# A 7x7 depthwise convolution taken image by image, as two matrix products for tiles of sixteen by two pixels

## The chip, the cores and the metric

One NeuronCore of one Trainium2 chip runs the whole program. The metric is the device time of one execution in microseconds (us). Engines: TensorE (PE; its weight loads are PEld), VectorE (DVE), ScalarE (ACT), GpSimd (POOL), and SyncE (SP), which here only issues transfers.

## The reference, cut to what matters

The input `x` is 4 images of 256 channels and 64 x 64 pixels, in float32. Two layers follow each other, each added to its input. Layer A is an attention whose keys and values come from a 2x2 convolution with stride 2. Layer B is an attention within each quarter of an image (16 rows, 1024 pixels), to which a 7x7 convolution of the values is added before the last projection:

```python
def _L1_conv_ref(x, w_qkv, b_qkv, w_pe, b_pe, w_proj, b_proj):
    ...
    qkv = _conv1x1(x, w_qkv, b_qkv)            # q, k, v: 8 heads of 32
    ...
    attn = softmax(einsum('bihd,bjhd->bhij', q, k) * scale)   # in one quarter
    out = einsum('bhij,bjhd->bihd', attn, v)
    ...
    out = out + _dwconv7(v_full, w_pe, b_pe)   # each channel by itself, 7 x 7
    return _conv1x1(out, w_proj, b_proj)

x = x + _L0_conv_ref(_gn(x), ...)              # layer A
x = x + _L1_conv_ref(_gn(x), ...)              # layer B
```

## The kernel before, in words

**Units and steps.** The work is written as a sequence of 128 units: 16 for each of the 8 pairs of layer and image, first A for images 0 to 3, then B for images 0 to 3. So layer A is units 0 to 63, layer B of image b is units 64 + 16b to 79 + 16b. A unit is 4 heads by 512 queries. It has 8 steps, one for each 128 keys; there are 1024 steps. Each step is the same on TensorE: four products for the scores (`s`, line 261), and the four weighted sums (`av`, line 272) of the step before. ScalarE makes two exponentials of 128 x 1024 in each step (line 265), VectorE adds up the exponentials for the divisors (line 797). Once in a unit, four `den` products (line 281) make the divisors, and GpSimd's transfers carry their reciprocals.

**Side work.** Everything else is hung on this frame. `at(g, j, f)` calls `f` in unit g, step j. Work of TensorE is queued with `task(parts, f)`: a generator cut in parts. After its own products, each step takes one part from this first-in-first-out queue (two if more than 7 parts wait, three beyond 14, and one less where j is 2). `need` takes parts ahead of time where a result is wanted at once. The order of all engines' instructions is that of this program (`manual_schedule`), SP's transfers included: an instruction at the head of an engine's queue that waits holds all that stand behind it.

**Values.** `plan_values(b, c)` makes the values of eight rows of image b: it loads `hv`, normalizes it on ScalarE, multiplies (`vals_ps`, two tasks of two parts), and adds the bias on ScalarE into `vout`. `vout` goes to HBM twice: as `vala` for attention (read as `vc`, and transposed on VectorE by `make_v`), and as `vals`, rows of all four images side by side with a margin of zeros.

**The convolution.** `plan_conv(n)` takes four channels of all four images. Its matrices are bands: the vertical taps are in the 126 x 32 matrix (42 rows of the image for each of three horizontal shifts; `BAND`, `BROWS`), and three such products cover seven columns. It loads six pieces of `vals` into `rows` (line 705), for every second n three pieces of `bands` (line 717), and does 24 products of 256 columns (line 732) in three parts. `HD` is 32: each product fills 32 columns of the array, and four of them, m = 0 to 3, stand beside each other. The result is copied by ScalarE (`cout`, line 739) and stored in `conv` (line 741). The convolutions wait for the values of all images: they are due at `begin` = unit 70.5 and every 0.52 units, 64 in all.

**The projections.** Therefore the attention output of images 0 to 2 is stored (`attd`, line 548), and read back with `conv` (lines 556 and 562) from unit 105.3 on, every 0.8 units: `add_conv` adds both on VectorE (line 572), and `project` (two tasks of two parts, `ops`) multiplies and adds the residual `xm` (line 583). For image 3 it follows attention directly.

Of the kernel before, what the change touches and what calls it, by code (L numbers as in the profile page):

```python
# [15 lines left out]
P = 128  # L16
# [17 lines left out]
BAND = HH // 2 + 2 * HALO  # L34
BROWS = 42
TC = 8
# [18 lines left out]
def direct_path(  # L55
# [31 lines left out]
    attd = [[dram.tile([P, CT, CH], FP, name=f"attd_{b}_{c}") for c in range(NCH)] for b in range(B - 1)]  # L87

    vals = dram.tile([HH + 2 * HALO + BROWS - BAND, C, B, XP], FP, name="vals")

    vala = [[dram.tile([4, HD, NH, 4, XP], FP, name=f"vala_{b}_{a}") for a in range(NAREA)] for b in range(B)]
    conv = dram.tile([C, B, N], FP, name="conv")

    bands = dram.tile([C // TC, 9, BROWS + HH // 2 - 1, TC], FP, name="bands")
# [369 lines left out]
    def plan_b(b, u):  # L464
# [13 lines left out]
        def make_k(a, qd, half):  # L478
            if qd == 0 and half == 0:
                kvs["k"] = k_tile(("B", b, a))  # L480
            k, ps = kvs["k"], ps_side(f"k1ps_{b}_{a}_{qd}_{half}")
            for t in range(CT):
                product(
                    ps, lhsT=wqkv_sb[:, t, 1, qd * P : (qd + 1) * P],
                    rhs=hs[a][:, t, half * CH : (half + 1) * CH], start=(t == 0), stop=(t == CT - 1),
                )
                if t == 0:
                    yield

            S.activation(  # L490
                k[:, qd, :].rearrange("p (j t i) -> p t j i", t=4, i=32)[:, 2 * half : 2 * half + 2],
                ps.rearrange("p (t j i) -> p t j i", t=2, i=32), AF.Identity, bias=bqkv_sb[:, 1, qd : qd + 1],
            )
            if qd == 1 and half == 1:
                ks["B", b, a] = k

        def load_v(a, half):
            vcs[a, half] = pool.tile([P, NH // 2, 4, XP], FP, tag="vc", name=f"vc_{b}_{a}_{half}", bufs=2)
            nc.sync.dma_start(
                vcs[a, half], vala[b][a][:, :, half * NH // 2 : (half + 1) * NH // 2].rearrange("t c h r x -> (t c) h r x")  # L500
            )

        def make_v(a, half):

            if half == 0:
                kvs["v"] = v_tile(("B", b, a))
            v, vc = kvs["v"], vcs.pop((a, half))
            V.transpose(
                out=v[:, :, half * P : (half + 1) * P].rearrange("p (r j) (h c) -> p h r j c", j=2, c=HD),
                in_=vc[:, :, :, HALO : HALO + WW].rearrange("p h r (j w) -> p h r j w", w=HD),  # L510
            )
            if half == 1:
                vs["B", b, a] = v
# [17 lines left out]
        for a in range(NAREA):  # L531
# [6 lines left out]
            for half in range(2):  # L538
                at(g - 3, 2 + 5 * half, lambda a=a, half=half: load_v(a, half))
                at(g - 2, 2 + 4 * half, lambda a=a, half=half: make_v(a, half))  # L540
# [5 lines left out]

        def store_att(c):
            nc.sync.dma_start(attd[b][c], atts.pop(("B", b, c)))
# [5 lines left out]
        def load_rest(c):  # L554
            cv = chunk_tile(f"cv_{b}_{c}")
            nc.sync.dma_start(cv, conv[:, b, c * CH : (c + 1) * CH].rearrange("(t p) n -> p t n", p=P))
            att = None
            if c == NCH - 1:
                load_residual(c)
            if b < B - 1:  # L560
                att = chunk_tile(f"at_{b}_{c}")
                nc.sync.dma_start(att, attd[b][c])
            rest[c] = cv, att

        def add_conv(c):
            cv, att = rest[c]
            if c < NCH - 1:
                load_residual(c)
            if att is None:
                att = atts["B", b, c]  # L570
            for t in range(CT):
                V.scalar_tensor_tensor(cv[:, t, :], cv[:, t, :], bpe_sb[:, t : t + 1], att[:, t, :], ALU.add, ALU.add)

        def project(c, to):
            cv, ps = rest[c][0], ps_side(f"ops_{b}_{c}_{to}")
# [7 lines left out]
            V.scalar_tensor_tensor(xm[:, to, :], ps, bproj_sb[:, to : to + 1], xm[:, to, :], ALU.add, ALU.add)  # L583
# [4 lines left out]

        for c in range(NCH):
            g, j = u + 2 * c + 3, 5  # L590
            if b < B - 1:
                at(g, j + 1, lambda c=c: store_att(c))
                g, j = 0, int(NKT * (late + spread * (b * NCH + c)))
            else:
                at(g, j, lambda c=c: add_conv(c))
                at(g, j + 2, lambda c=c: soon_tasks([(2, project, c, to) for to in range(CT)]))
                g, j = (g - 1, 5) if c < NCH - 1 else (g - 2, 2)
            at(g, j, lambda c=c: load_rest(c))
            if b < B - 1:
                at(g, j + 4, lambda c=c: add_conv(c))  # L600
                at(g, j + 6, lambda c=c: soon_tasks([(2, project, c, to) for to in range(CT)]))
# [13 lines left out]

    def plan_zeros(g):


        def zeros():
            zero = pool.tile([P, 8 * B * XP], FP, tag="rows", name="zero", bufs=2)  # L620
            V.memset(zero, 0.0)
            for lo, hi in ((0, 3), (67, 71), (71, 74)):
                nc.sync.dma_start(
                    vals[lo:hi].rearrange("r c b x -> (r c b x)").rearrange("(p n) -> p n", n=8 * B * XP),
                    zero[: (hi - lo) * C // 8],
                )
            flat = bands.rearrange("k x i c -> (k x i c)").rearrange("(p n) -> p n", p=P)
            nc.sync.dma_start(flat, zero[:, : flat.shape[1]])

        def taps():  # L630
            tap = pool.tile([NTAP, C], FP, tag="cout", name="tap", bufs=2)
            nc.sync.dma_start(tap, wpe.rearrange("c k -> k c"))
            for n in range(7):
                nc.sync.dma_start(
                    bands[:, :7, BAND - 1 - n, :].rearrange("k x c -> x k c"),
                    tap[7 * n : 7 * n + 7, :].rearrange("x (k c) -> x k c", c=TC),
                )

        at(g, 0, zeros)
        at(g, 2, taps)  # L640
# [3 lines left out]
    def plan_values(b, c, start):  # L644
# [10 lines left out]
        def values(t):  # L655
            if t == 0:
                vout = made["v"] = pool.tile([P, CT, RC, XP], FP, tag="rows", name=f"vout_{b}_{c}", bufs=2)
                V.memset(vout[:, :, :, :HALO], 0.0)
                V.memset(vout[:, :, :, HALO + WW :], 0.0)
            h, vout = made["h"], made["v"]  # L660
            ps = ps_side(f"vals_ps_{b}_{c}_{t}")
            for tt in range(CT):
# [7 lines left out]
                vout[:, t, :, HALO : HALO + WW], ps.rearrange("p (r w) -> p r w", w=WW), AF.Identity,  # L670
                bias=bqkv_sb[:, 2, t : t + 1],
            )
            if t == CT - 1:
                stored[b, c] = True
                for n in range(2):
                    for tt in range(CT):
                        nc.sync.dma_start(
                            vala[b][c // 2][2 * (c % 2) + n, :, 4 * tt : 4 * tt + 4].rearrange("c h r x -> h c (r x)"),
                            vout[:, tt, 4 * n : 4 * n + 4, :].rearrange("p r x -> p (r x)"),
                        )  # L680
                for r in range(RC):
                    nc.sync.dma_start(
                        vals[HALO + HH - 1 - c * RC - r, :, b, :].rearrange("(t p) x -> p t x", p=P), vout[:, :, r, :]
                    )
# [8 lines left out]
    band_tiles = {}  # L693

    def plan_conv(n, start):

        made = {}

        def load():
            row, size = C * B * XP, 4 * B * XP  # L700
            need(stored, (B - 1, NCH - 1))
            made["x"] = xs = pool.tile([3 * BROWS, 2, 4, B, XP], FP, tag="rows", name=f"rows_{n}", bufs=2)
            for half in range(2):
                for s in range(3):
                    nc.sync.dma_start(
                        xs[s * BROWS : (s + 1) * BROWS, half].rearrange("p c b x -> p (c b x)")[:, : size - s],
                        bass.AP(
                            tensor=vals.tensor, offset=vals.offset + (1 - half) * (HH // 2) * row + n * size + s,
                            ap=[[row, BROWS], [1, size - s]],
                        ),  # L710
                    )
            k, part = divmod(4 * n, TC)
            if part == 0:
                band = band_tiles[k] = pool.tile([3 * BROWS, 3, HH // 2, TC], FP, tag="band", name=f"band_{k}", bufs=2)
                step = (BROWS + HH // 2 - 1) * TC
                for s in range(3):
                    nc.sync.dma_start(
                        band[s * BROWS : (s + 1) * BROWS].rearrange("p g y c -> p g (y c)"),
                        bass.AP(
                            tensor=bands.tensor, offset=bands.offset + (9 * k + s) * step,  # L720
                            ap=[[TC, BROWS], [3 * step, 3], [1, HH // 2 * TC]],
                        ),
                    )

        def convolve():
            xs, (k, part) = made.pop("x"), divmod(4 * n, TC)
            ps = ps_side(f"conv_ps_{n}").rearrange("p (i b x) -> p i b x", i=2, b=B)
# [716 lines left out]
```

## Time and profile before

| | us |
|---|---|
| median of 3 runs (lowest to highest) | 3266.19 (3265.86 to 3269.84) |
| the profiled execution, as timed | 3270.47 |
| its span, first to last instruction | 3268.7 |
| TensorE busy, 29730 matmul records | 3218.2 |
| ScalarE busy | 2525.6 |
| VectorE busy | 2491.6 |
| GpSimd busy | 487.2 |

A float32 matmul of the program appears as two records, so a part of eight products is 16 records. `128*32` is rows by columns of the weights. A row of the timeline shows: start in us, length in us, engine, line, operation, tiles, shape, how many records, and in brackets the idle time before it and what ended it. A row of the windows shows, for a stretch of time, the busy us of each engine and its number of instructions, then the granted share of TensorE's clock, the busy share of the 16 DMA engines, and GB/s.

### The profile page before, as it was taken

Reading aid. Unit: us, or ns where it says so; the run is one execution under the profiler, and the core shown is the slowest. Engines: PE = TensorE matmul, PEld = TensorE weight load, DVE = VectorE, ACT = ScalarE, POOL = GpSimd, SP = SyncE. Lnnn points to the kernel's source line nnn. Section 1 sums busy time; section 2 is a strip of 40 time slices with the busy share of each in tenths; the row PEclk is TensorE's granted clock in tenths of the full one; section 3 lists DMA queues with packets and bytes.
Section 4 is the critical chain, followed back from the end, with each engine's and each line's share of the span. In section 5 each row is a group of like instructions: output and inputs, shape, how many; then the busy total and the mean of one; then the engine's idle time right before and its main releaser. Section 6 shows DMA issues by size and latency. Waiting matters only on the chain.

```text
span 3268.7 us, 72561 instructions
## 1 busy us (share of the span) xinstructions
PE 3218.2 (98%) x29730; PEld 961.1 (29%) x29730; DVE 2491.6 (76%) x2621; ACT 2525.6 (77%) x2993; POOL 487.2 (15%) x923
## 2 busy tenths in 40 slices
PE   7999999999999999999999999999999999999997
PEld 4233323333233322222222333333333322222221
DVE  3777897779877787778876767666776778888887
ACT  3888788887888888888887777777777787776765
POOL 0111121111211111111111111111111111111111
PEclk9999999999999999999999999999999999999999
DMA  5312212313322213553236667676766643445431
GB/s 179 80 64 73 77 66 90 100 59 116 100 69 84 65 63 91 148 138 113 82 120 158 162 151 178 159 174 141 180 171 153 172 142 123 166 147 172 155 121 57
DMA packets 319853, 397.27 MB, mean 122 GB/s; under 512 B 182652, under 2 KB 215708, under 8 KB 319192
## 3 DMA queue, kind: packets, MB, share of 16 engines
q1 hardware_dynamic: 291064, 356.06, 38.5%
q0 software_dynamic: 28448, 36.48, 4.2%
q8 instruction: 236, 3.87, 0.5%
q14 instruction: 105, 0.86, 0.1%
HBM read 285.98 MB, written 106.42 MB: 120 GB/s over the span
## 4 chain that ended last, share of the span: by engine, by line
PE 94%; DMA 2%; issue 1%; ACT 1%; DVE 1%; SPq 0%; POOL 0%; DVEq 0%; ACTq 0%; POOLq 0%
PE s L261 33%; PE av L272 29%; PE conv_ps L732 5%; PE den L281 4%; PE k0ps L155 3%; PE k1ps L155 3%; PE q1ps L155 3%; PE v0ps L155 3%; PE q0ps L155 3%; PE ops L155 3%; PE vals_ps L155 3%; ACT p L265 1%; DVE p L797 1%; DMA conv<-cout 0%; DMA rows<-vals 0%
## 5 line engine op out<-in xcount | busy, mean ns | idle before, releaser
L797 DVE TENSOR_TENSOR p<-p 128x1024 f32<-128x1024 f32 x1792 | 2113.3, 1219 | 623.1 <-ACT p L265 583.3
L265 ACT ACTIVATE p<-s 128x1024 f32<-128x1024 f32 x2048 | 2016.9, 1027 | 571.9 <-PE s L261 564.0
L261 PE MATMUL s<-q,k_A 32*128 32x512 f32 x4096 | 608.2, 640 | 1.4 <-ACT p L265 0.9
L261 PE MATMUL s<-q,k_B 32*128 32x512 f32 x4096 | 588.7, 640 | 1.1 <-ACT p L265 0.8
L272 PE MATMUL av<-p,v_A 128*32 128x512 f32 x4096 | 551.1, 603 | 0.0
L272 PE MATMUL av<-p,v_B 128*32 128x512 f32 x4096 | 546.0, 604 | 0.0
L308 POOL DMA_DIRECT2D rb<-recs x508 | 252.4, 502 | 454.1 <-DMA recs<-few 377.5
L306 POOL DMA_DIRECT2D recs<-few x127 | 70.2, 553 | 1423.2 <-DVE sums L305 1372.1
L261 PEld LDWEIGHTS s<-q,k_A 32*128 32x128 f32 x4096 | 176.3, 183 | 357.8 <-issue 273.3
L261 PEld LDWEIGHTS s<-q,k_B 32*128 32x128 f32 x4096 | 162.5, 182 | 363.3 <-issue 290.5
L272 PEld LDWEIGHTS av<-p,v_A 128*32 128x32 f32 x4096 | 89.4, 108 | 383.0 <-issue 335.0
L272 PEld LDWEIGHTS av<-p,v_B 128*32 128x32 f32 x4096 | 87.6, 108 | 378.8 <-issue 332.9
L732 PE MATMUL conv_ps<-rows,band 126*32 126x256 f32 x3072 | 195.1, 379 | 0.0
L732 PEld LDWEIGHTS conv_ps<-rows,band 126*32 126x32 f32 x3072 | 123.0, 139 | 113.0 <-issue 78.3
L297 POOL DMA_DIRECT2D rows<-den_sb x127 | 74.6, 587 | 433.3 <-ACT den_sb L290 424.1
L281 PE MATMUL den<-p,ones 128*32 128x512 f32 x1024 | 137.8, 605 | 0.4 <-DVE p L797 0.4
L155 PE MATMUL ops<-cv,wp_sb 128*32 128x512 f32 x1024 | 129.8, 600 | 6.0 <-issue 6.0
L155 PE MATMUL vals_ps<-hv,wqkv_sb 128*32 128x512 f32 x1024 | 130.1, 596 | 3.9 <-ACT vout L669 3.8
L155 PE MATMUL k0ps<-taps,wk_sb 128*32 128x256 f32 x2048 | 130.6, 383 | 3.0 <-ACT taps L243 3.0
L155 PE MATMUL k1ps<-h,wqkv_sb 128*32 128x512 f32 x1024 | 128.7, 593 | 2.4 <-ACT cout L739 1.6
L155 PE MATMUL q0ps<-hq,wq_sb 128*32 128x512 f32 x1024 | 129.8, 592 | 0.0
L155 PE MATMUL q1ps<-h,wqkv_sb 128*32 128x512 f32 x1024 | 129.7, 596 | 0.1
(87 smaller groups left out, 1594.9 us busy)
## 6 DMA issues: line engine op xcount, KB each, us to landing
rb<-recs POOLq DMA_DIRECT2D x508, 64.0 KB, 2.4
rows<-vals SPq DMA_DIRECT2D x128, 189.0 KB
rows<-vals SPq DMA_DIRECT2D x128, 188.8 KB
rows<-vals SPq DMA_DIRECT2D x128, 188.7 KB
vala<-vout SPq DMA_DIRECT2D x128, 144.0 KB
vals<-vout SPq DMA_DIRECT2D x256, 72.0 KB
vc<-vala SPq DMA_DIRECT2D x32, 576.0 KB
hq<-in_x SPq DMA_DIRECT2D x32, 512.0 KB
```

The lines of the kernel that those rows point to most:

```text
L155: T.matmul(out[cols, :], lhsT=lhsT[:, cols], rhs=rhs, start=start, stop=stop)
L261: T.matmul(pairs[h // 2][:, h % 2, :], lhsT=k[rows, unit[0], j * P : (j + 1) * P], rhs=q[rows, :], start=True, stop=True,)
L265: exps = [lambda i=i: S.activation(p[i], pairs[i], AF.Exp, scale=SCALE) for i in range(2)]
L272: T.matmul(av[HD * h : HD * h + HD, :], lhsT=v[:, j, unit[0] * P + HD * h : unit[0] * P + HD * h + HD], rhs=p[h // 2][:, h % 2, :], start= ...
L281: T.matmul(dens[g][HD * h : HD * h + HD, :], lhsT=ones, rhs=p[h // 2][:, h % 2, :], start=True, stop=True,)
L297: G.dma_start(rows, den_sb[0:P:HD, :])
L306: G.dma_start(recs.rearrange("h (q n) -> (h q) n", n=CH // HD), few[:, 1, :])
L308: G.dma_start(rb[HD * h : HD * h + HD, :], recs[h : h + 1, :].to_broadcast([HD, CH]))
L732: T.matmul(ps[HD * m : HD * m + HD, i], lhsT=band_tiles[k][:, g, :, part + c], rhs=xs[:, m % 2, c, :, 3 * g : 3 * g + WW], start=(g == 0), ...
L797: soon(1, lambda i=i: V.tensor_add(ps[0][i], ps[0][i], ps[j][i]))
```

## The change

The convolution is done for one image at a time. A product now makes tiles of sixteen rows by two columns (`TY`, `TX`; 32 pixels, so again 32 columns of the array): its 88 rows hold 22 image rows, by two even/odd columns, by two shifts. Two products cover 22 rows and 8 columns of input. One n is 16 channels of one image: 32 products of 128 columns, in two parts. `vals` of each image holds even and odd columns apart (`f`), and so do `vala`, the keys and `conv`. The matrices are built once in HBM (`mats`, by 8 reads and one store for each of 32 k) and read for each image; `load_rows` reads two of them and eight pieces of `vals` for one n. It is called for n + 1 at the end of `convolve(n)`, behind the copy of the result and its store. `conv` is read by 16 transfers for each chunk of eight rows. The projections of all images follow their attention, as those of image 3 did; `attd` is gone. The values are stored for each 128 channels by themselves, in `vc` buffers, of which there are five; they and the convolutions have new due times.

```diff
-BAND = HH // 2 + 2 * HALO
-BROWS = 42
-TC = 8
+TY, TX, NY, XT, NP, TC = 16, 2, 4, WW // 2 + 4, 88, 8
+BY, BX = 2 * 16 + 5, 2 + 7
...
-        def load_v(a, half):
-            vcs[a, half] = pool.tile([P, NH // 2, 4, XP], FP, tag="vc", name=f"vc_{b}_{a}_{half}", bufs=2)
...
+        def load_v(a, n):
+            vcs[a, n] = pool.tile([P, 2, 4 * TX, XT], FP, tag="vc", name=f"vc_{b}_{a}_{n}", bufs=5)
...
         def load_rest(c):
             cv = chunk_tile(f"cv_{b}_{c}")
-            nc.sync.dma_start(cv, conv[:, b, c * CH : (c + 1) * CH].rearrange("(t p) n -> p t n", p=P))
...
+            for y in range(c * RC, (c + 1) * RC):
+                n, r = y // TY, TY - 1 - y % TY
+                for t in range(CT):
+                    nc.sync.dma_start(
+                        cv[:, t, :].rearrange("p (f r x) -> p r f x", f=TX, r=RC)[:, y - c * RC],
+                        conv[b][t * P : (t + 1) * P, r * TX : (r + 1) * TX, n, :],
+                    )
...
-            if b < B - 1:
-                at(g, j + 1, lambda c=c: store_att(c))
-                g, j = 0, int(NKT * (late + spread * (b * NCH + c)))
...
+            at(*((g - 1, 5) if b < B - 1 or c < NCH - 1 else (g - 2, 2)), lambda c=c: load_rest(c))
+            at(g, j, lambda c=c: add_conv(c))
+            at(g, j + 2, lambda c=c: soon_tasks([(2, project, c, to) for to in range(CT)]))
...
+        def matrices(k):
+            band = pool.tile([NP, 2, TY, TX * TC], FP, tag="band", name=f"made_{k}", bufs=2)
+            for dc in range(TX + 6):
+                p = NP // 2 * (dc // 2 % 2) + dc % 2
+                nc.sync.dma_start(
+                    band[p : p + 2 * (TY + 6) - 1 : 2, dc // 4],
...
+            nc.sync.dma_start(mats[k], band)
...
+            at(g + 2, 3 * k, lambda k=k: matrices(k))
...
-                vout = made["v"] = pool.tile([P, CT, RC, XP], FP, tag="rows", name=f"vout_{b}_{c}", bufs=2)
...
+            vout = pool.tile([P, RC, TX, XT], FP, tag="vc", name=f"vout_{b}_{c}_{t}", bufs=5)
...
+    def load_rows(b, n):
+        for c in range(NCH):
+            need(stored, (b, c))
+        loaded[b, n] = made = []
+        row, size = C * XT, 8 * XT
+        for k in (2 * n, 2 * n + 1):
+            band = pool.tile([NP, 2, TY, TX * TC], FP, tag="band", name=f"band_{b}_{k}", bufs=2)
+            xs = pool.tile([NP, 2, NY, 8, XT], FP, tag="rows", name=f"rows_{b}_{k}", bufs=2)
+            made.append((band, xs))
+            nc.sync.dma_start(band, mats[k])
+            for a in range(4):
+                p = NP // 2 * (a % 2)
+                nc.sync.dma_start(
+                    xs[p : p + NP // 2, a // 2].rearrange("p y c x -> p y (c x)")[:, :, : size - 3],
+                    bass.AP(
+                        tensor=vals[b].tensor, offset=vals[b].offset + k * size + a,
+                        ap=[[row, NP // 2], [TY * TX * row, NY], [1, size - 3]],
+                    ),
+                )
...
+    def convolve(b, n):
+        size = NY * WW // TX
+        ps = ps_side(f"conv_ps_{b}_{n}")
+        for k, (band, xs) in enumerate(loaded.pop((b, n))):
+            if k:
+                yield
             for i in range(2):
-                for g in range(3):
+                for half in range(2):
                     for m in range(4):
...
                         T.matmul(
...
+                            lhsT=band[:, half].rearrange("p y (x c) -> p (y x) c", c=TC)[:, :, 4 * i + m],
+                            rhs=xs[:, half, :, 4 * i + m, : WW // TX], start=(half == 0), stop=(half == 1),
                         )
...
+        S.copy(out.rearrange("p i y -> p (i y)"), ps)
+        nc.sync.dma_start(
+            conv[b][16 * n : 16 * n + 16].rearrange("(i c) m y x -> (c m) i (y x)", i=4), out
+        )
+        if n + 1 < C // 16:
+            load_rows(b, n + 1)
+        yield
...
-        at(0, when, load)
-        at(0, when + 4, lambda: task(3, convolve))
...
+        if n == 0:
+            at(0, when - 8, lambda: load_rows(b, n))
+        at(0, when, lambda: task(2, convolve, b, n))
...
-            plan_values(b, c, ends[b] + 1.8 + (14.5 if b == 1 else 0) + (3.4, 1.0, 1.6, 0.4)[b] * c)
-    for n in range(C // 4):
-        plan_conv(n, begin + pace * n)
+            plan_values(b, c, (17.8, 42, 54.5, 67)[b] + (2.0, 1.5, 1.3, 2.2)[b] * c)
+        for n in range(C // 16):
+            plan_conv(b, n, (36, 58, 75.5, 93.5)[b] + (1.36, 1.06, 1.1, 1.1)[b] * n)
```

## The prediction

> **What bounds the kernel now.** First the page: engines, then the chain of work that ended last.
>
> ```profile
> span 3268.7 us, 72561 instructions
> PE 3218.2 (98%) x29730; PEld 961.1 (29%) x29730; DVE 2491.6 (76%) x2621; ACT 2525.6 (77%) x2993; POOL 487.2 (15%) x923
> ...
> PE 94%; DMA 2%; issue 1%; ACT 1%; DVE 1%; SPq 0%; POOL 0%; DVEq 0%; ACTq 0%; POOLq 0%
> ```
>
> TensorE is the bound, and the other two compute engines have a quarter of the span free. Busy overstates TensorE, so I read the price of side work off the timeline, from one `s` group to the next. TensorE in layer B, then three rows of a stretch without side work:
>
> ```profile
> 2190.46 1.14 PE L261 MATMUL s<-q,k_B 32*128 32x512 f32 x8
> ...
> 2192.41 1.92 PE L732 MATMUL conv_ps<-rows,band 126*32 126x256 f32 x32
> 2194.26 1.14 PE L261 MATMUL s<-q,k_B 32*128 32x512 f32 x8
> ...
> 2196.22 1.06 PE L732 MATMUL conv_ps<-rows,band 126*32 126x256 f32 x16
> 2197.20 1.14 PE L261 MATMUL s<-q,k_B 32*128 32x512 f32 x8
> ```
> ```profile
> 3212.04 1.31 PE L261 MATMUL s<-q,k_B 32*128 32x512 f32 x8
> ...
> 3214.28 1.14 PE L261 MATMUL s<-q,k_B 32*128 32x512 f32 x8
> ...
> 3216.35 1.31 PE L261 MATMUL s<-q,k_B 32*128 32x512 f32 x8
> ```
>
> A step with two convolution parts takes 3.80 us, with one 2.94, with none 2.07 to 2.24: **a part costs 0.87 us**, and 192 of them 167 us. In an empty step ScalarE's two exponentials (2 x 1.03 us) set the pace. Thus time is nearly a count of parts, plus the waits of TensorE.
>
> How a product's time is made, by the tile view of `conv_ps` (count, then shortest, median and longest ns):
>
> ```profile
> L732 PEld LDWEIGHTS conv_ps<-rows,band x3072: 135/138/164, 1797.9 to 2653.0; 126*32 126x32 f32 x192
> L732 PE MATMUL conv_ps<-rows,band x3072: 377/379/435, 1797.9 to 2653.2; 126*32 126x256 f32 x192
> ```
>
> Four products stand beside each other, so a part (16 records) is four groups of 0.218 us for 256 columns. The longest, 435 ns, is 56 over the median: I read it as a group whose weights were not loaded ahead.
>
> How fast a load comes: SP's timeline, and the windows over the same load (1.13 MB of `rows`, 0.39 MB of `band`):
>
> ```profile
> 2218.71 2.45 SPq L705 DMA_DIRECT2D rows<-vals  x6
> 2221.21 1.37 SPq L717 DMA_DIRECT2D band<-bands  x3
> ```
> ```profile
> 2218.70:2220.00 1.30, 1.30 (x12) 0.35 (x16) 1.30 (x2) 1.30 (x3) 0.00 (x0) 1.00 0.29 53
> ...
> 2222.00:2223.00 1.00, 1.00 (x12) 0.16 (x8) 1.00 (x2) 0.48 (x2) 0.00 (x0) 1.00 0.83 193
> ...
> 2226.00:2227.00 1.00, 1.00 (x20) 0.60 (x16) 0.32 (x1) 0.99 (x2) 0.00 (x0) 1.00 0.96 209
> 2227.00:2228.00 1.00, 1.00 (x20) 0.35 (x12) 0.00 (x0) 1.00 (x2) 0.00 (x0) 1.00 0.30 47
> ```
>
> The last two columns say it: a slow first 1.3 us, then some 200 GB/s until about 2227. Its matmuls begin at 2229.37, 10.7 us after the first issue, without a wait. Last, what a stall costs beyond itself:
>
> ```profile
> 1281.45 1.94 PE L155 MATMUL vals_ps<-hv,wqkv_sb 128*32 128x512 f32 x8 [3.15 <-ACT vout L669]
> 1283.32 1.67 PE L261 MATMUL s<-q,k_A 32*128 32x512 f32 x8
> ```
>
> After the wait, eight records take 1.94 us instead of 1.04, and the next group 1.67 instead of 1.14: about 1.5 us more.
>
> [...]
>
> **The change, part by part.**
>
> *Convolution products.* 192 parts of four 256-column groups go; 128 parts of eight 128-column groups come (4 images x 16 n x 2). If columns set the time, a group takes half of 0.218, a part again 0.87 us: 64 x 0.87 = **56 us less**. A load of 56 ns fits under a group of 109 ns. No group this short is in the trace. If weights lay fully bare, 1024 groups x 56 ns = 57 us would come back and nothing be saved; a faster side I exclude, since columns and clock stay. I take 56. The steps left without side work, counted in both program orders, are 88 and 84: 4 x 0.17 = 0.7 us less.
>
> *The load behind the convolution.* New: `load_rows(b, n + 1)` stands in SP's queue behind the copy and store of `convolve(n)`. In the changed program's order, the 64 blocks' first part stands this many steps behind its load: 0 for three blocks, 1 for one, 2 for two, 3 for one, 4 or more for 57. Before, load and task were planned four steps apart. Counting from the step's start: copy 0.6 and store issue 0.65, with their hand-overs 1.4 us. A k brings 0.18 MB of `mats` and 0.80 MB of `vals`; at 200 GB/s that is 4.9 us, and fixed 2.1 (1.3 as above, 0.8 after the last byte: a 64 KB `rb` lands in 2.4 us on the page, of which 0.3 is its bytes). So the first k is there at 8.4 us, the second at 13.3. TensorE comes to the part 1.95 us into its step. Same step: 6.4 us of waiting, then 2.0 more at the second part, 8.4 x 3 = 25 us. One step: 3.5 + 2.0. Two steps: 0.6 + 4.0 where both parts stand in one step, else 0.6. Three or more: none. Sum 36 us; with five clock drops of 1.6, **44 us more**. Behind the waiting product are the next scores, and so ScalarE and everything. Ends: nothing, if these steps come late[...]. I take 44.
>
> *Values.* `vout` gets five buffers for two. TensorE's weight loads of `vals_ps` waited 9.9 us for `vout`, and products behind `cout` 1.6 (waits): **11 us less**. Late next would be the same buffers, shared with `vc`: ends 0 and 15 less.
>
> *SP's queue.* The order counts 1418 transfers before, 2143 after; `rows` takes a median of 0.38 us to issue. (a) `conv` for a chunk: 16 x 0.38 = 6 us plus landing, with 4 to 11 steps (12 us and more) until VectorE needs it; ten buffers of `p` cover some lateness. (b) `matrices`: nine issues 3.5 us, then the store waits some 2 us for the reads, every three steps (8.8 us) in units 4 to 14, where `xa` and `hq` loads queue behind it with 4 or 5 steps of lead. (c) `attd` and its reads, 48 transfers, go. All this is covered by lead unless SP runs late: 0 to 15 us, I take **4 more**.
>
> *VectorE and ScalarE.* The sums by column (128 of 0.75 us), twice as many memsets and half-size transposes, the even/odd reads in `vout` and the keys (128 of 0.69). Were the strided ones twice as slow, either engine would gain some 90 us and still stand under 81% of the span: hidden by TensorE, except four at the very end, 0 to 3 us. I take 0. Keys, projections and values keep their number of products; 64 copies of `cout` stay 64.
>
> Sum: -56 - 1 + 44 - 11 + 4 = **-20 us** on the profiled execution's 3270.5 (span 3268.7 and 1.8 around it), so 3250.5. That execution is 4.3 above the median of 3266.2: **3247**.
>
> **The rivals.**
>
> *R1, slower: the load comes late.* At 140 GB/s the wait is 76 us: -56 - 1 + 76 - 11 + 4 = +12, 3278. [...] It decides from 71 us of waiting on, just under 9 us for a first k.
>
> *R2: weights show.* The short groups wait for their weights: +57 on the forecast, 3304; half of it, 3275. For it: 56 ns is half of the 109. Against: in the 256-column groups nothing of it is seen.
>
> *R3: the load is in time.* If the tight blocks wait less than 10 us in all, -56 - 1 + 10 - 11 + 4 = -54, 3212. For it: TensorE may reach those steps late. Against: the ones in the same step have less than 2 us.
>
> *R4: nothing is saved for want of filler*, since empty steps are paced by ScalarE: 64 parts would then have to leave empty steps, but these do not grow (88 to 84). It would give 3266 less the values' 11, and I give it little.
>
> **How the numbers follow.** Forecast 0.50, 3215 to 3262, nearly all faster; R1 0.20; R2 0.12; R3 0.13; R4 and others 0.05. A measurement of this kernel tells apart about 0.2%, 6.5 us. Faster: 0.48 + 0.13 + a little of the rest, 0.62; the same, the edge between forecast and R1, 0.14; slower 0.24. The range takes in R3's 3212 with 5 us to spare and most of R2: 3207 to 3290.
>
> **What would show it.** Right: `conv_ps` has 4096 records and some 135 us busy; `conv_ps` waits for DMA `rows`, about 36 us on fewer than ten occasions, in units 71, 87, 95 and 107 above all; no wait for `vout`; steps with one part still 2.94 us. Wrong: one-part steps of 3.1 us or more (R2); waits for `rows` under 10 us (R3) or over 70 (R1); ScalarE waiting for `xa` or `hq`, which I priced at 4 us.

## The result, and the profile after

| | before, us | after, us |
|---|---|---|
| median of 7 runs (lowest to highest) | 3269.4 (3265.9 to 3272.3) | 3287.5 (3281.0 to 3300.5) |
| the profiled execution, as timed | 3270.5 | 3287.5 |
| its span | 3268.7 | 3285.4 |
| granted TensorE clock, mean | 0.997 | 0.987 |

The changed kernel is **slower by 0.6%**: ratio 1.0061, 95% interval 1.0043 to 1.0080. The forecast was 3247, faster by 20 us; it came 18 slower. Its own runs lie up to 20 us apart, so a difference of a few us from it is not told apart.

The page of after: the engines, the chain that ended last by engine, and the group of the convolution's products.

```profile
span 3285.4 us, 75646 instructions
...
PE 3182.4 (97%) x30754; PEld 965.8 (29%) x30754; DVE 2508.6 (76%) x2717; ACT 2524.9 (77%) x2993; POOL 491.2 (15%) x923
...
PE 87%; DMA 6%; issue 2%; DVE 2%; ACT 1%; SPq 1%; POOL 0%; DVEq 0%; ACTq 0%
...
L742 PE MATMUL conv_ps<-rows,band 88*32 88x128 f32 x4096 | 143.0, 282 | 44.9 <-DMA rows<-vals 44.8
```

TensorE is busy 36 us less and the span is 17 us longer: the work went down, the waiting went up. The last two lines say where to look first. TensorE's share of the chain fell from 94% to 87%, that of transfers rose from 2% to 6%, and the convolution's products stood still for 44.8 us for `rows`. The tile view of `conv_ps` (count, then shortest, median and longest ns) shows the products themselves: a median of 272 ns at 128 columns, where before had 379 at 256.

```profile
L742 PEld LDWEIGHTS conv_ps<-rows,band x4096: 135/138/178, 969.4 to 2870.2; 88*32 88x32 f32 x196
L742 PE MATMUL conv_ps<-rows,band x4096: 270/272/432, 969.8 to 2870.3; 88*32 88x128 f32 x196
```

On the timeline, groups of four products follow each other every 0.109 us, half of the 0.218 of 256 columns and as forecast, and a step with one convolution part takes 2.94 us, as before.

**Where the time went.** For both traces I took each step from its first `s` product to the next step's, and counted what it takes over the usual time of a step with the same side work. This puts each stall under the step in which it falls:

| us over the usual, steps with | before | after | difference |
|---|---|---|---|
| convolution | 0.3 | 63.3 | +63.0 |
| divisors (`den`) | 3.0 | 16.9 | +13.9 |
| projections (`ops`) | 0.0 | 11.3 | +11.3 |
| values | 10.6 | 6.1 | -4.5 |
| keys, queries | 14.2 | 7.0 | -7.2 |
| nothing beside, others | 7.6 | 4.7 | -2.9 |
| sum | 35.7 | 109.3 | +73.6 |

From the first step's start to the last's it is 3152.9 before and 3169.5 after, 16.6 more. So without the stalls the steps became 57.0 us shorter (73.6 less 16.6), which is what 64 parts fewer should give (56 + 1 in the forecast). The gain was there; stalls of 74 us took it back.

The waits of after (total, times, longest) name three of them:

```profile
DVE st_A L338 <- DMA xs<-in_x: 33.8, 10, 7.9
...
PE den L283 <- DVE p L806: 10.6, 4, 5.5
...
PEld conv_ps L742 <- DMA rows<-vals: 7.3, 4, 2.0
```

With the 44.8 us of the products this makes 52.1 us for `rows`, on 21 occasions. VectorE's wait for `xs` was 10.3 us before. The wait of the values' weight loads for `vout` fell from 9.9 us to 2.4, none longer than 0.7.

**The longest stall, unit 71.** TensorE's timeline, SP's over the same time (start, length; SP's length is the time to issue), and ScalarE's copy:

```profile
1855.09 1.14 PE L263 MATMUL s<-q,k_B 32*128 32x512 f32 x8
...
1868.94 0.66 PE L742 MATMUL conv_ps<-rows,band 88*32 88x128 f32 x8 [11.72 <-DMA rows<-vals]
1871.36 1.52 PE L742 MATMUL conv_ps<-rows,band 88*32 88x128 f32 x24 [1.76 <-DMA rows<-vals]
1872.81 2.09 PE L263 MATMUL s<-q,k_B 32*128 32x512 f32 x8
```
```profile
1849.47 4.27 SPq L688 DMA_DIRECT2D vala<-vout  x2
1853.79 1.78 SPq L696 DMA_DIRECT2D vals<-vout  x2
1855.62 2.72 SPq L665 DMA_DIRECT2D hv<-xmid  x1
...
1858.91 0.37 SPq L751 DMA_DIRECT2D conv<-cout  x1
1859.39 0.40 SPq L722 DMA_DIRECT2D band<-mats  x1
```
```profile
1856.28 0.58 ACT L750 COPY cout<-conv_ps 128x512 f32<-128x512 f32 x1
```

The copy behind which the load stands ends 1.8 us into the step, at 1856.86: ScalarE normalized an `h` first. SP reaches its store only at 1858.91, another 2 us later: it is still issuing the value stores and `hv`. That one `hv` takes 2.72 us to issue, where the median of its kind is 0.43. The first k's load then takes from 1859.39 to 1871.36, 12.0 us. The window in the middle of it (busy us of each engine, then clock, DMA share, GB/s):

```profile
1864.00:1866.00 2.00, 0.00 (x0) 0.00 (x0) 0.00 (x0) 0.00 (x0) 0.00 (x0) 0.50 0.95 327
```

All engines stand still, the transfers are at 95%, and the granted clock is 0.50; the scores behind the wait then take 2.09 us instead of 1.14. The clock drops in the forecast's term were of this kind: over the 1.95 us behind the wait of 3.15 us in before (from 1281.45 on) the granted clock was 0.50, too.

**The same block without value stores ahead of it**, unit 87, TensorE and SP:

```profile
2280.19 1.14 PE L263 MATMUL s<-q,k_B 32*128 32x512 f32 x8
...
2287.88 0.66 PE L742 MATMUL conv_ps<-rows,band 88*32 88x128 f32 x8 [5.56 <-DMA rows<-vals]
2289.87 1.52 PE L742 MATMUL conv_ps<-rows,band 88*32 88x128 f32 x24 [1.32 <-DMA rows<-vals]
```
```profile
2281.40 0.40 SPq L722 DMA_DIRECT2D band<-mats  x1
```

SP is in time here. The first k is complete 8.5 us after its first issue; the second, by the next such row at 2295.63, after 14.2. The forecast had 7.0 and 11.9.

### The profile page after: what moved, and what is told of

Its sections match the earlier page's. It is cut to its first block, busy times and chain, and to the rows that moved or that the text cites. A ratio compares the mean times of both kernels' runs of the same rounds, so it can differ in the third digit from the quotient of the medians.

```text
span 3285.4 us, 75646 instructions
## 1 busy us (share of the span) xinstructions
PE 3182.4 (97%) x30754; PEld 965.8 (29%) x30754; DVE 2508.6 (76%) x2717; ACT 2524.9 (77%) x2993; POOL 491.2 (15%) x923
## 4 chain that ended last, share of the span: by engine, by line
PE 87%; DMA 6%; issue 2%; DVE 2%; ACT 1%; SPq 1%; POOL 0%; DVEq 0%; ACTq 0%
PE s L263 31%; PE av L274 27%; PE den L283 4%; DMA rows<-vals 4%; PE conv_ps L742 3%; PE ops L157 3%; PE k0ps L157 3%; PE q0ps L157 3%; PE v0ps L157 3%; PE k1ps L157 3%; PE vals_ps L157 3%; PE q1ps L157 3%; DVE p L806 1%; ACT p L267 1%; DMA xm<-xmid 0%
## 5 line engine op out<-in xcount | busy, mean ns | idle before, releaser
L263 PE MATMUL s<-q,k_B 32*128 32x512 f32 x4096 | 599.0, 645 | 0.0
L742 PE MATMUL conv_ps<-rows,band 88*32 88x128 f32 x4096 | 143.0, 282 | 44.9 <-DMA rows<-vals 44.8
L742 PEld LDWEIGHTS conv_ps<-rows,band 88*32 88x32 f32 x4096 | 126.6, 140 | 117.7 <-issue 106.0
L283 PE MATMUL den<-p,ones 128*32 128x512 f32 x1024 | 142.3, 608 | 10.6 <-DVE p L806 10.6
L157 PE MATMUL ops<-cv,wp_sb 128*32 128x512 f32 x1024 | 135.1, 606 | 10.9 <-issue 6.4
L300 POOL DMA_DIRECT2D few<-rows x127 | 72.6, 571 | 480.2 <-DMA rows<-den_sb 473.7
```

The lines of the kernel that those rows point to most:

```text
L157: T.matmul(out[cols, :], lhsT=lhsT[:, cols], rhs=rhs, start=start, stop=stop)
L263: T.matmul(pairs[h // 2][:, h % 2, :], lhsT=k[rows, unit[0], j * P : (j + 1) * P], rhs=q[rows, :], start=True, stop=True,)
L283: T.matmul(dens[g][HD * h : HD * h + HD, :], lhsT=ones, rhs=p[h // 2][:, h % 2, :], start=True, stop=True,)
L300: G.dma_start(few[:, 0, :], rows.rearrange("h (q n) -> (h q) n", n=CH // HD))
L742: T.matmul(ps[HD * m : HD * m + HD, (2 * k + i) * size : (2 * k + i + 1) * size].rearrange("p (y x) -> p y x", y=NY), lhsT=band[:, half].r ...
```

## The experiments

Each time stands beside runs of the kernel before on the same chip (medians 3269.2 to 3269.4). "Less than after" sets it against the 3287.5 of the changed kernel, which was not run again beside them. What is said of stalls is read from one kept trace of each kernel.

### Convolutions at the front of TensorE's queue

```diff
-        at(0, when, lambda: task(2, convolve, b, n))
+        at(0, when, lambda: soon_tasks([(2, convolve, b, n)]))
```

`soon_tasks` puts the block right behind the task at the queue's head and ahead of all others, so the blocks come at the pace of their due times, and none stands less than four steps behind its load. The other tasks come later by the parts that now go first.

> The changed kernel with one edit: a convolution's task goes to the front of the side queue instead of its end. In its program order no block stands less than 4 steps behind its load (before the edit: 0, 0, 0, 1, 2, 2, 3 for the seven tightest). Loads, bytes, products and parts stay. Theory 1, the distance between load and use: the steps with convolution parts, which lie 67 us above their usual length in the changed kernel's trace, lose nearly all of it (under 10 us left), and the time falls by some 55 us, to 3225 to 3240. Theory 2, SyncE is late in any case (stores of the values in front of the load): about half of the waiting stays, 3250 to 3265. Theory 3, the transfers as such are too many: the waiting moves to other tiles, 3280 to 3290.

Measured: 3227.6 us, ratio 0.9876 (0.9861 to 0.9891), 60 us less than after. In the kept trace, the fastest of four runs and 9 us under their median, the stalls of convolution steps fell from 63.3 to 6.3 us, and no product waits for `rows` any more. The mean clock of the four is 0.995 to 0.997, for 0.987 in after. So the late load is **shown** as the cause of some 57 us: blocks bunched up by the first-in-first-out queue, each with its load chained to the end of the block before.

### Matrices at half the pace

```diff
-            at(g + 2, 3 * k, lambda k=k: matrices(k))
+            at(g + 2, 6 * k, lambda k=k: matrices(k))
```

> The changed kernel with one edit: the 32 matrices are built every 6 steps instead of every 3, in units 4 to 28 instead of 4 to 16. Theory 1, SyncE is full while they are built (eight reads of 0.78 us and a store in 8.8 us), so that xs comes late, VectorE waits for it, and den for VectorE: the den steps at units 12, 14 and 16, 13 us above their usual length, go back to 2.93 us, and the time falls by 10 to 15 us, to 3272 to 3277. Rival, these den steps wait for the divisors of GpSimd's queue, which the matrices do not touch: 3285 to 3290.

Measured: 3276.7 us, ratio 1.0022 (1.0014 to 1.0030), 11 us less than after. In the kept trace the stalls at `den` fell from 16.9 to 4.8, and VectorE's waits for `xs` from 33.8 to 13.3. How they come about is seen in after, at unit 12: SP, VectorE, TensorE.

```profile
350.03 0.40 SPq L103 DMA_DIRECT2D xs<-in_x  x1
350.48 6.60 SPq L643 DMA_DIRECT2D made<-bands  x8
358.69 0.32 SPq L650 DMA_DIRECT2D mats<-made  x1
```
```profile
354.08 1.29 DVE L338 BATCH_NORM_STATS2 st_A<-xs 128x6 f32<-128x512 f32 x2 [6.58 <-DMA xs<-in_x]
```
```profile
372.60 2.11 PE L283 MATMUL den<-p,ones 128*32 128x512 f32 x6 [5.50 <-DVE p L806]
```

The eight reads of a matrix take 6.6 us to issue, and the store behind them, which needs their bytes, is issued at 358.7, 1.6 us after the last of them; with it a matrix costs SP over 8 us, as much as the three steps it is planned for (8.8 us). SP is late with `xs`, VectorE waits for it with the sums of `p` behind, and after some steps the divisors wait for VectorE. A new stall of 8 us came in at unit 20, step 5, where the slower matrices now meet the first value stores: the queue's load was moved nearly as much as spread.

### Both together

> Both edits: convolution tasks at the front of the side queue, and matrices every 6 steps. If the two causes are apart, the gains add: 65 to 80 us, 3208 to 3225, which is under the kernel before by 1.3 to 1.9%. If both are one shortage of SyncE, they do not add: 3225 to 3245.

Measured: 3223.2 us, ratio 0.9857 (0.9842 to 0.9872). That is 64 us less than after, where the two alone make 60 and 11. The intervals are too wide to say whether the gains add: the time lies in the first range of the expectation, 2 us from the second. The stall at unit 20 stays, with 7.4 us.

### Loads of 48 rows instead of 44

```diff
-TY, TX, NY, XT, NP, TC = 16, 2, 4, WW // 2 + 4, 88, 8
+TY, TX, NY, XT, NP, TC = 16, 2, 4, WW // 2 + 4, 96, 8
```

With it, two more rows of zeros for each image, a memset of each matrix, and 9% more bytes in each load. The question is whether a load with more rows comes sooner.

> The changed kernel with 48 instead of 44 rows in each half of the pieces of vals and of the matrices (the four added rows of the matrices are zero; 9% more bytes). [...] a first half is there after some 6.6 us instead of 8.5, the second after 10.5 instead of 14.2; the convolution's waits fall from 67 to about 40 us, 3258 to 3268. Rival, [...]: 3283 to 3293.

Measured: 3286.1 us, ratio 1.0053 (1.0040 to 1.0067), the same as after. At unit 87 the first k was complete after 7.4 us instead of 8.5, and over the five tight blocks the stalls are 9% less. Windows over the load, from 1.6 us after its first issue on, in after and in this run:

```profile
2283.00:2285.00 2.00, 0.00 (x0) 0.00 (x0) 2.00 (x3) 1.43 (x2) 0.00 (x0) 1.00 0.65 201
2285.00:2287.00 2.00, 0.00 (x0) 0.00 (x0) 1.56 (x2) 0.00 (x0) 0.00 (x0) 1.00 0.71 176
```
```profile
2287.74:2289.74 2.00, 0.00 (x0) 0.00 (x0) 2.00 (x3) 1.43 (x2) 0.00 (x0) 0.97 1.06 263
2289.74:2291.74 2.00, 0.18 (x4) 0.21 (x8) 1.56 (x2) 0.00 (x0) 0.00 (x0) 0.50 1.10 211
```

The transfers' busy share, the mean of the two windows, rose from 0.68 to 1.08. The bytes per us rose by a quarter only, from 188 to 237 GB/s: a packet of 1140 bytes took 86 ns (median over the run) instead of 66. So more rows brought this load sooner, by less than the busy share rose. How many engines served it, no view shows. The small gain went back at `den`, 28.2 us instead of 16.9; I didn't separate whether the added memsets and zeros did that.

### Without the value stores of images 2 and 3

```diff
-            for f in range(TX):
+            for f in range(TX if b < 2 else 0):
...
-                        tensor=vals[b].tensor, offset=vals[b].offset + k * size + a,
+                        tensor=vals[b % 2].tensor, offset=vals[b % 2].offset + k * size + a,
```

> The changed kernel, order of products and loads untouched, but the values of images 2 and 3 are not stored to vals, and their convolutions read the vals of images 0 and 1: 64 of 128 stores of 1024 pieces of 144 bytes are left out, which stand in SyncE's queue in front of the tight loads of units 64 and 71 (steps 515 and 573). Theory 1, the tight blocks wait longer than worked out because SyncE is late behind these stores: the blocks at 573 and 515, 17 and 12 us in the changed kernel, come down to the 10 us of the undisturbed ones (units 87 and 95) and 6 us, and some 10 us of smaller waits near values go; time 3262 to 3272. Rival, the loads are slow by themselves: those two keep their waits, 3281 to 3290.

The kernel leaves out the stores to `vals` alone; those to `vala` stay. Measured: 3272.3 us, ratio 1.0009 (1.0002 to 1.0016), 15 us less than after. Unit 71 again, TensorE and SP:

```profile
1854.81 0.67 PE L742 MATMUL conv_ps<-rows,band 88*32 88x128 f32 x8 [6.32 <-DMA rows<-vals]
```
```profile
1848.15 0.37 SPq L751 DMA_DIRECT2D conv<-cout  x1
```

The wait is 6.3 us instead of 11.7. SP issues the store 1.8 us after the step's start instead of 3.8, and the load takes 8.3 us instead of 12.0: the stores had held SP, and I read the rest as their bytes in the load's way. The stores had slowed the issues behind them, too: the longest issue of a `conv` store was 3.04 us in after and is 0.55 here.

### The load ahead of the copy

```diff
+        if n + 1 < C // 16:
+            load_rows(b, n + 1)
         out = pool.tile([P, 4, size], FP, tag="cout", name=f"cout_{b}_{n}", bufs=2)
...
-        if n + 1 < C // 16:
-            load_rows(b, n + 1)
```

> The changed kernel with load_rows(b, n + 1) called ahead of the copy and its store in convolve(n), all else as it was. Theory 'chain behind the copy': in a tight block the load is issued about 1.0 us earlier (0.6 us of copy and 0.4 us of the store's issue); seven blocks, 6 to 8 us less, 3280 against 3287. Rival 'the queue in front decides': SP arrives late at the load by its value stores and chunk loads, nothing moves but the two or three undisturbed blocks, 0 to 3 us less, 3285.

Measured: 3263.3 us, ratio 0.9984 (0.9978 to 0.9991), 24 us less than after: three times what I expected. SP and TensorE at unit 87:

```profile
2263.40 0.32 SPq L722 DMA_DIRECT2D band<-mats  x1
...
2268.90 0.38 SPq L753 DMA_DIRECT2D conv<-cout  x1
```
```profile
2262.28 1.06 PE L742 MATMUL conv_ps<-rows,band 88*32 88x128 f32 x32
...
2266.21 1.14 PE L263 MATMUL s<-q,k_B 32*128 32x512 f32 x8
...
2270.63 0.99 PE L742 MATMUL conv_ps<-rows,band 88*32 88x128 f32 x24 [1.71 <-DMA rows<-vals]
```

The load starts at 2263.40, 2.8 us **before** the step of 2266.21 in which it stood behind the copy until now. All it needs is a free buffer, and the first k's buffer comes free with the first part of the block before (2262.28 to 2263.34), a step earlier than the copy. SP had run ahead of the program, up to the first transfer that had to wait; in the change that was the store of `cout`, and the load was held behind it.

The five tight blocks in these runs (us over the usual, the step and its next; the kept trace of the last column is its fastest run, 4 us under the median):

| unit | forecast, with clock | after | no value stores | load ahead of copy |
|---|---|---|---|---|
| 71 | 10.0 | 17.2 | 10.9 | 12.7 |
| 64 | 6.2 | 11.6 | 7.0 | 12.0 |
| 87 | 10.0 | 10.4 | 10.4 | 4.7 |
| 95 | 10.0 | 9.9 | 11.2 | 5.1 |
| 107 | 7.1 | 7.6 | 7.2 | 3.8 |

The table tells two causes apart. At 71 and 64, in the time of image 2's and 3's value stores, leaving those out brings the forecast back; at 87, 95 and 107 it does nothing, and moving the load ahead of the copy halves the stall.

### The load in two halves

```diff
+            if n + 1 < C // 16:
+                load_rows(b, n + 1, k, 1)
```

This stands at the end of each part, in place of one load behind the store.

> The changed kernel with the load cut in two: the first k of block n + 1 is loaded right behind the first part's products of block n, the second k behind the second part's, both ahead of the copy and its store. Theory 'distance in steps': where the two parts of block n stand in different steps, the first load gets one step of 2.9 us more and the second k's load overlaps less with it; blocks whose parts share a step gain only the 1.0 us of copy and store. 12 to 20 us less, 3267 to 3275 against 3287. Rival 'one load's own time': the two halves share the transfers' rate, the second k is late instead of the first, and it gains no more than leaving the copy ahead does, 3280 or more.

Measured: 3262.0 us, ratio 0.9973 (0.9965 to 0.9981). That is 25 us less than after and one less than the run above. Neither theory has it: it gains more than the first's 12 to 20 us, but the cut adds nothing clear to what the place ahead of the copy gives. I read that as SP already starting at each buffer's release there, as unit 87 shows.

### The residual's load ahead of the chunk's

```diff
             cv = chunk_tile(f"cv_{b}_{c}")
+            load_residual(c)
```

Two kernels, both with the convolutions at the front and a matrix every fourth step; the first also loads `xm` at the head of `load_rest`, and not in `add_conv`.

> Convolution tasks at the front of the side queue; matrices every 4 steps (done by unit 20, before most values); the residual xm loaded ahead of the 16 pieces of conv instead of behind the convolution's loads. If SyncE's order is what is left, the waits of VectorE for xm (7 to 11 us) and for xs go, and the time is 3208 to 3218; if what is left belongs to VectorE's own order (the sums by column take 1.15 us instead of 0.75), 3220 to 3226, as with matrices every 6 steps.

> As the last, without the edit on xm: tells what the pace of 4 steps does by itself, and so what xm is worth. Expected 3215 to 3225; xm worth 4 to 8 us.

Measured: 3222.3 us with it (ratio 0.9853, 0.9839 to 0.9868), 3227.0 without (0.9869, 0.9855 to 0.9883). The 5 us aren't where I looked for them. VectorE's waits for `xm` to land, 12.6 us without it, are gone with it, and yet projection steps stall 14.4 us with it and 11.4 without. The difference lies mainly in one convolution step at unit 78, 9.0 us without and 2.8 with, where ScalarE waits 6.5 us for `hv` with the exponentials behind. So the residual's place is not shown to matter. The first of these and "both together" are within each other's runs and the fastest here, **1.4 to 1.5% faster than before**.

### Sums without the step by columns

```diff
-                    by_column(cv[:, t, :]), by_column(cv[:, t, :]), bpe_sb[:, t : t + 1],
-                    att[:, t, :].rearrange("p (q f) -> p q f", f=TX), ALU.add, ALU.add,
+                    cv[:, t, :], cv[:, t, :], bpe_sb[:, t : t + 1], att[:, t, :], ALU.add, ALU.add,
```

> The kernel with both the queue's front and every sixth matrix, in which add_conv adds the convolution without the order by columns (each sum then pairs other pixels than the reference's). It asks where seven waits of 0.8 to 0.9 us for VectorE's xm in steps with a projection come from, 6 us in all. Theory 'stepped sums': a sum of 128x512 falls from 1.15 to 0.75 us, 64 of them 26 us less of VectorE, VectorE comes to xm in time, the waits go, 3217 against 3223. Rival 'VectorE's queue of sums of exponentials': the waits stand behind those sums (1.22 us each) whatever the convolution's sums take, and the time stays at 3223.

Measured: 3222.4 us, ratio 0.9855 (0.9838 to 0.9873), the same as "both together". VectorE's groups by form, first after, then this run:

```profile
L573 DVE SCALAR_TENSOR_TENSOR cv<-cv,bpe_sb,att_B 128x512 f32<-128x512 f32 x64 | 68.1, 1146 | 0.0
```
```profile
L573 DVE SCALAR_TENSOR_TENSOR cv<-cv,bpe_sb,att_B 128x512 f32<-128x512 f32 x64 | 45.1, 745 | 0.0
```

The step by columns costs a sum 0.40 us, and the span nothing that shows. Five of the seven waits of 0.8 to 0.9 us in projection steps are still there, and the last two fell to 0.3; VectorE's sums of `p` stand ahead of `xm`.

### Products of 64 columns

The kernel with the convolutions at the front, each product cut in two of 64 columns, weights loaded for each; timed once.

> As e1_front, but each convolution product of 128 columns is cut into two of 64 columns, with the weights loaded for each: same columns, twice the products and weight loads. It asks at what length the weights (56 ns where they lie bare) begin to show. If they hide while they are shorter than the columns' time (54 ns): one-part steps of 2.95 to 3.05 us instead of 2.94. If weights and columns add: 16 groups of 110 ns, a part of 1.76 us, steps of 3.8 us. If a fixed cost for each instruction rules, in between, 3.2 to 3.5.

Measured: 3243.1 us. The tile view:

```profile
L743 PEld LDWEIGHTS conv_ps<-rows,band x8192: 135/151/171, 951.5 to 2815.7; 88*32 88x32 f32 x200
L743 PE MATMUL conv_ps<-rows,band x8192: 217/227/278, 951.8 to 2815.7; 88*32 88x64 f32 x200
```

Groups follow each other every 63 ns (median), so a part is 16 x 63 ns = 1.0 us, and a step with one part is 3.10 us, between the ranges expected. Half of 109 would be 54.5: at 64 columns some 9 ns a group show, of the weights or of another cost, which this run doesn't separate. At 128 columns a group takes half of the 218 ns of 256, so there nothing of the weights shows. This takes the second rival away.

## Why the prediction was wrong

**Products: right.** 56 + 1 forecast, 57.0 by the steps, with 0.109 us a group and 2.94 us a step. R2, the weights, and R4, no filler, fall with it.

**Values: right**, by its own sign and bounds: 11 forecast, 0 to 15; the steps with values, keys, queries and nothing beside lost 14.6 together. I give that to the buffers of `vout` only in part: its wait fell by 7.5 us, the rest was not tried.

**The load behind the convolution: the mechanism right, the size not.** Units 71, 87, 95 and 107 stalled, and R3, the load in time, falls. The term was 44 and measured 63. Three of the five tight blocks came within half a us of the working, in part by luck: a first k took 8.5 us and not 7.0, but TensorE could begin on its first half after 6.5 us (2287.88 in unit 87), so that the slower load cost little. What failed is the sentence "Counting from the step's start: copy 0.6 and store issue 0.65": it took ScalarE and SP as idle at that moment. At unit 71 the copy ended 1.8 us into the step, and SP, still issuing value stores and `hv`, reached its store at 3.8. At unit 64 the store's issue alone took 2.40 us behind value stores, where the median is 0.38:

```profile
1647.39 2.40 SPq L751 DMA_DIRECT2D conv<-cout  x1
```

These two blocks make 13 of the 19 us, and leaving the stores out took 15 us off the time. The smaller late ones (units 59, 66, 81), which I had at nothing, make most of the rest.

**SP's queue: the step that failed.** It was priced at 4 us, 0 to 15, and came to about 19: 13.9 at `den` and 5 at the projections. The price of an issue was wrong in (b): I took 0.38 us from `rows`, and the reads of `bands`, 64 bytes a piece, take 0.78. Nine issues at 0.38 fit a slot of 8.8 us with 3 to spare; at 0.78, and with the wait for their bytes (1.6 us at unit 12), they fill it. I had named the right sign of it (loads of layer A behind the matrices), but looked for the wait on ScalarE, for `xa` and `hq`; it was VectorE's, for `xs`. Half the pace took 11 us off. The 5 us are one wait for `xm` at unit 70 (6.5 us on VectorE), which was issued behind a convolution's load.

**VectorE at the projections: 0 forecast, 6 measured,** in seven waits of under a us for VectorE. "I take 0" for VectorE and ScalarE was right on the stepped sums, to within the 1.2 us that two of these waits lost without them, and wrong on the rest. What makes VectorE late at those seven steps, other than its sums of `p` ahead of `xm`, stays open.

**R1, the slower rival,** had the sign (3278 for 3287), and little of its reason. It rested on a load at 140 GB/s, an assumption of mine that no trace of before shows. At unit 87 the load moved some 188 GB/s over 4 us, near the forecast's 200, with the transfers busy for 0.65 to 0.71. With 48 rows that load took 7.4 us instead of 8.5. R1's deciding point, 71 us of waiting on `rows`, was not reached: 52 us of waits and 63 us with what they cost beyond. R1's sum was passed because of the other lateness, which I had kept at 4 in every case. That the errors of one queue add up in several terms was in no rival.

**Sum:** -57 + 63 - 15 + 14 + 11 = +16, against 16.6 by the steps. It closes by construction, since the 57 is what the stalls leave over. Between the -20 of the forecast and this lie 19 us in the load's term, 15 in SP's, 6 in VectorE's, and 4 that the values gave back.

## What to carry to other kernels

A load issued behind a result's store in the same in-order queue started when that store could start, not when its own buffer was free; moving it ahead of the store was worth 24 us here. So put loads ahead of stores that wait, and count, in the order of the program, the steps between a load and its use, with the queue's other work in between. Read the price of an issue from a transfer of the same kind with the same transfers ahead of it, not from a neighbour's row (0.78 us for the reads of `bands`, where `rows` had 0.38), and add up what a queue has to issue in each planned slot. Due times that look even are not, if the tasks go through a first-in-first-out queue: one line that keeps their spacing turned 0.6% slower into 1.2% faster.

## What was not expected of the hardware

- The time to issue a transfer on SP differed with its pieces: 0.38 us for a median load of `rows` (176 pieces of 1140 bytes), 0.78 us for a read of `bands` with 352 pieces of 64 bytes; a value store with 1024 pieces of 144 bytes had a median of 0.89 us and a longest of 5.1 us.
- It also differed with what stood ahead in the queue: an `hv` load has a median of 0.43 us and took 2.72 behind value stores, and the longest issue of a `conv` store fell from 3.04 us to 0.55 when half of the stores to `vals` were left out.
- The load of 1140-byte rows at unit 87 was complete about an eighth sooner with 48 rows than with 44 (7.4 us for 8.5), with 9% more bytes; its packets were slower each (86 for 66 ns), and the transfers' busy share was 1.08 for 0.68.
- A sum on VectorE that takes even and odd columns in turn from where they lie apart in SBUF took 1.15 us instead of 0.75; the one that reads PSUM in such steps took the same as before (748 and 749 ns).
- Groups of four products side by side, weights loaded for each, followed each other every 218 ns at 256 columns, 109 at 128, and 63 at 64.
